# Rebuilding the set-up of a four-layer image kernel: core tables without a DRAM round trip, g on four row groups, small transfers first, aggregations per group of images

## The chip, the cores and the metric

The kernel runs on one core of a Trainium2 chip. Its time is the device time of one execution in microseconds (us), a median over runs. TensorE (PE) multiplies, VectorE (DVE), ScalarE (ACT) and GpSimd (POOL) work elementwise, and SyncE (SP) only issues transfers; ACT and POOL issue some as well. The order of the instructions on each engine is the one written in the kernel.

## The reference

The input `x` is 1024 images of 16 x 16 pixels and 16 channels, in float32. Four layers follow each other, each of the form `x = x + layer(group_norm(x))`, with 8 groups of two channels. Only the start of the first layer concerns this change:

```python
# _gn: mean and variance of an image's group (16 x 16 x 2 values)
x = x + _L0_conv_ref(_gn(x), core0, core1, core2)
# for each core r,o,i,k: einsum('roik,brix->bkox'); ranks 1,16,16,1; all dims 16
```

Layer 0 is thus one 4096 x 4096 matrix applied to every image, and that matrix is given by three small tensors: `core0` (16 x 16 x 16 values: o, i, k), `core1` (16 x 16 x 16 x 16) and `core2` (16 x 16 x 16). Layers 1 and 3 are a perception step with two dense layers, layer 2 is a 3 x 3 convolution.

## The kernel before, in words

The images are worked on in two sets of 512 (n = 0 and 1). Layer 0 runs on TensorE as 128 x 128 float32 matrices times 512 images. The matrix is cut into 2 x 2 blocks, which take seven products instead of eight (`PRODUCTS`), and the work is five phases of 16 units; phase 0 makes two products per unit of the first quarter with the first 512 images alone, and the second 512 images are read, turned and normalised beside it.

For a unit u the matrix `w` is built like this. `g` is the contraction of `core1` with `core2`; it is computed once, stored in DRAM (`g_dram`), and `gload(u)` reads 4 x 32 KB of it into `gq` (two buffers). `build(u)` multiplies `gq` with `R`, a table that spreads `core0` over partitions, on four groups of 32 rows (the `pw` matmuls), and ACT copies the four results into `w`. `mix(u, i)` adds parts of `w` on DVE for the products of phase 0 only the first of these. `pieces(u, k)` are the large matmuls `po`; between them it issues `build(u + 1)`, `gload(u + 2)` and the store of unit u - 1 (`m_dram`), so the order on all engines follows PE's.

The set-up ahead of phase 0 has two strands.

The input strand: SP loads x as eight 1 MB pieces (two halves of the rows, four groups of 128 images each; line 822). DVE takes `bn_stats` of each piece (line 834, eight instructions for a piece) and, in `small` (line 865), 32 `bn_aggr`. Then follow a square root on ACT, five small instructions (`newton`), two sets of four copies (`widen`, line 881), PE transposes of both (`spread`, `ptmr`, line 889), and ACT copies into `mr`. `normed` (line 911) subtracts the mean and multiplies by the reciprocal deviation, eight DVE instructions of 128 x 1024 for the first part. `turn` (line 840, `ptin`) transposes the images themselves, four transposes a row, and POOL stores the rows in DRAM as `xr` (lines 845 and 853).

The table strand (`train_setup`): ACT issues sixteen transfers of 16 KB for `core1` and one each for `core2` and `core0`. `cores` transposes `core1` in 32 transposes of 16 columns (line 522) into 16 partitions and `core0` in two. `sums` writes `core0` in masked form to DRAM (`c_dram`) and reads it back four times as `R`. `gs` multiplies 16 partitions of `core1` with `core2` (line 561, 32 matmuls for the first half of g), ACT copies (line 565), SP stores (line 570).

A transfer on SP's or ACT's path takes one of eight completion semaphores in turn, and waits at its issue until the former user of that semaphore has landed. So an issue on SP can wait for a transfer that ACT issued.

The order around the start is written out by hand:

```python
now(setup[:1])
now(stat[0] + stat[1] + lines[0][:4] + setup[1:] + tail[:1]
    + lines[1][:4] + tail[1:] + lines[0][4:10])
start, phases = layer_train()
start()          # gload(0), gload(1), build(0), mix(0, i), fetch(0)
now(normed(0, 0, 1) + combined(0, True))
```

Of the kernel before, what the change touches and what calls it, by code (L numbers as in the profile page):

```python
# [9 lines left out]
F32 = mybir.dt.float32  # L10
# [9 lines left out]
P = 128  # L20
# [83 lines left out]
def conv_preact_kernel(ctx: ExitStack, tc: tile.TileContext, a: dict, out: bass.AP):  # L104
# [31 lines left out]
    def work(shape, tag, name, dt=F32):  # L136
        p, sizes = pool["sb"]
        return p.tile(shape, dt, tag=tag, name=name, bufs=sizes[tag])
# [330 lines left out]
    c_dram = dram.tile([2, 16, 512], F32, tag="c_dram", name="c_dram")  # L469
# [27 lines left out]
    def train_setup(room):  # L497

        c1t = room[0:16, 0:4096].rearrange("p (h i w a k) -> p h i w a k", h=2, i=S, w=4, a=2)
        ra = [room[0:16, 4096 + 512 * a2 : 4608 + 512 * a2].rearrange("p (s m b f) -> p s m b f", s=2, m=2, b=2) for a2 in range(2)]  # L500
        c0 = room[0:16, 5888:6144].rearrange("p (i o) -> p i o", o=S)
        c1n = work([P, 2, NB], "t4", "core1")[:, 0].rearrange("p (t f) -> p t f", t=2)
        r = work([P, NB], "n", "cores")
        c2 = r[0:16, 0:256]
        c0n = r[:, 256:288].rearrange("p (t k) -> p t k", t=2)

        core1 = a["L0_conv_core1"].rearrange("k o i q -> o k (i q)")
        for h in range(2):
            for wv in range(4):
                for a2 in range(2):  # L510
                    A.dma_start(c1n[32 * wv + 16 * a2 : 32 * wv + 16 * a2 + 16, h], core1[8 * a2 + 4 * h + wv])
        A.dma_start(c2, a["L0_conv_core2"].rearrange("r o i k -> r (o i k)"))
        A.dma_start(
            c0n, a["L0_conv_core0"].rearrange("r o i k -> (r o i) k").rearrange("(t p) k -> p t k", p=P)
        )

        def cores():
            for h in range(2):
                for i2 in range(0, S, 4):
                    pt = bank([16, 4, P], "w", "pc1")  # L520
                    for j in range(4):
                        T.transpose(pt[:, j], c1n[:, h, 16 * (i2 + j) : 16 * (i2 + j) + 16], ident)
                    A.copy(c1t[:, h, i2 : i2 + 4].rearrange("p i w a k -> p i (w a k)"), pt)
            pt = bank([16, 2, P], "w", "pc0")
            for t in range(2):
                T.transpose(pt[:, t], c0n[:, t], ident)
            for t in range(2):
                A.copy(
                    c0[:, :, 8 * t : 8 * t + 8].rearrange("p i o -> p o i"),
                    pt[:, t].rearrange("p (o i) -> p o i", i=S),  # L530
                )

        def sums():
            c = c0.rearrange("p (b s t) o -> p s b (t o)", b=2, s=2)
            for a2 in range(2):
                G.memset(ra[a2], 0.0)
                G.tensor_copy(ra[a2][:, :, a2], c)
                G.dma_start(c_dram[a2], ra[a2].rearrange("p s m b f -> p (s m b f)"))

            st0["R"] = work([P, 2, 256], "R", "R")  # L540
            for g in range(4):
                G.dma_start(
                    st0["R"][32 * g : 32 * g + 32].rearrange("p s f -> p (s f)"),
                    c_dram.rearrange("a k f -> (a k) f"),
                )

        def gs(h, ih, o, ni, tag):


            if (h, ih, o) not in st0:  # L550
                if ih:
                    g = work([P, 2, NB], "t4", "g")
                else:
                    if o == 0:
                        st0["gw"] = work([P, 28, P], "w", "g")
                    g = st0["gw"][:, 8 * o : 8 * o + 8]
                st0[h, ih, o] = [g.rearrange("p m f -> p (m f)").rearrange("p (o f) -> p o f", o=8), 0]
            g, i2 = st0[h, ih, o]
            pg = bank([P, ni, 8, S], tag, "pg")
            for j in range(ni):  # L560
                T.matmul(
                    pg[:, j], c1t[:, h, 8 * ih + i2 + j].rearrange("p w a k -> p (w a k)"),
                    c2[:, P * o : P * o + P], start=True, stop=True,
                )
            A.copy(
                g[:, :, 16 * i2 : 16 * (i2 + ni)].rearrange("p o (j i) -> p j o i", j=ni), pg
            )
            st0[h, ih, o][1] += ni
            if i2 + ni == 8:
                nc.sync.dma_start(  # L570
                    g_dram[ih, 2 * h : 2 * h + 2, :, :, 8 * o : 8 * o + 8].rearrange(
                        "w v k o f -> (w v k) o f"
                    ),
                    g,
                )

        def all_gs(ih, tag):
            return [
                (1, lambda h=h, o=o: gs(h, ih, o, 4, tag)) for h in range(2) for o in range(2) for _ in range(2)
            ]  # L580

        return [cores, sums] + all_gs(0, "w"), all_gs(1, "mw")


# [227 lines left out]
    def input_steps(n, tag, lag, queue):  # L812
# [23 lines left out]
        def turn(h, wh):  # L836
            pt = bank([P, 4, P], tag[0], "ptin")
            for bg in range(4):
                x = slots[:, 4 * (h // 8) + bg].rearrange("p (h w f) -> p h w f", h=8, w=2)
                T.transpose(pt[:, bg], x[:, h % 8, wh], ident)  # L840
            pt = pt.rearrange("p g b -> p (g b)")
            if wh == 0 and h % 8 < 4:
                A.copy(X[:, h // 8, h % 4, 1], pt)
                if h % 4 == 3:
                    G.dma_start(
                        xr[n][0, h - 3 : h + 1].rearrange("h p b -> p h b"), X[:, h // 8, :, 1]
                    )
                return
            if h % 2 == 0:
                st["l"] = work([P, 2, NB], "t4", "lines")  # L850
            A.copy(st["l"][:, h % 2], pt)
            if h % 2 == 1:
                G.dma_start(
                    xr[n][wh, h - 1 : h + 1].rearrange("h p b -> p h b"), st["l"]
                )

        def small():
            t = work([P, NB], "n", "small")
            st["mv"] = t[:, 0:64].rearrange("p (g k e) -> p g k e", g=4, k=8)
            st["ve"], st["t"], st["r"] = (  # L860
                t[:, 64 + 32 * j : 96 + 32 * j].rearrange("p (g k) -> p g k", g=4) for j in range(3)
            )
            for bg in range(4):
                for g in range(8):
                    V.bn_aggr(st["mv"][:, bg, g], st["b"][:, bg, g])
            V.tensor_scalar(st["ve"], st["mv"][:, :, :, 1], GN_EPS, None, ALU.add)
            A.activation(st["t"], st["ve"], AF.Sqrt)
# [23 lines left out]

        loads = [lambda half=half, bg=bg: load(half, bg) for half in range(2) for bg in range(4)]
# [6 lines left out]
        tail = [(3, small), 2, (1, newton), (1, lambda: widen(0)), (1, lambda: widen(1)), 1]  # L899
        tail += [(0, lambda: spread(0)), lag, (0, lambda: spread(1)), 2]  # L900
        return loads, stat, lines, tail

    def normed(p, n, src=None):

        X, E = part_tile(p)

        def op(b, t, k):
            x = X[:, b, t : t + 2, n]
            y = x if k or src is None else X[:, b, t : t + 2, src]
            m = mr[:, k, n].unsqueeze(1).broadcast_to([P, 2, NB])  # L910
            V.tensor_tensor(x, y, m, ALU.mult if k else ALU.subtract)  # L911

        return [(1.2, lambda b=b, t=t, k=k: op(b, t, k)) for b in range(2) for t in (0, 2) for k in range(2)]
# [76 lines left out]
    def layer_train():  # L990
# [147 lines left out]
        def start():  # L1138
            gload(0)
            gload(1)  # L1140
            build(0)
            for i in range(5):
                mix(0, i)
            fetch(0)
# [5 lines left out]
        return start, steps  # L1150
# [381 lines left out]
    with ExitStack() as es:  # L1532
        stage(es, dict(gn, w=2, r=2, gq=2, R=1), dict(o=3, w=4, m=1))
        setup, later = train_setup(XN[0].rearrange("p n b -> p (n b)")[:, 8192:14336])
        tag = ["w"]
        loads, stat, lines, tail = input_steps(0, tag, 0, nc.sync)
# [3 lines left out]
        now(setup[:1])  # L1540
        now(stat[0] + stat[1] + lines[0][:4] + setup[1:] + tail[:1] + lines[1][:4] + tail[1:] + lines[0][4:10])
        start, phases = layer_train()
        start()
        now(normed(0, 0, 1) + combined(0, True))
        tag[0] = "mw"
        late = lines[0][10:] + lines[1][4:]
        loads, stat, lines, tail = input_steps(1, tag, 2, G)
        woven_in = [x for j in range(2) for i in range(4) for x in stat[j][i : i + 1] + lines[j][4 * i : 4 * i + 4]]
# [88 lines left out]
```

## Time and profile before

| What | Value |
|---|---|
| median of 3 runs | 3057.21 us (3052.56 to 3057.89) |
| profiled execution | 3054.15 us |
| its span, first to last instruction | 3052.4 us |
| PE busy | 2982.6 us, 98% of the span |
| DVE, ACT, POOL busy | 58%, 36%, 22% |
| mean granted TensorE clock | 0.988 |
| first large matmul (line 1098) begins | 50.13 us into the span |

In the rows of the timeline the first number is the start in us from the span's start, the second the time that the piece took; then come engine, line, operation, output and inputs, shapes, and in brackets how long the engine had idled before it and what ended that. A float32 matmul leaves two records, a transpose one. "issue" means that the profile shows nothing that the engine waited for. In rows by stretch each engine has its busy time, PEclk is the clock that TensorE was granted as a share of full speed, and the DMA share is the mean busy share of the 16 DMA engines.

### The profile page before, as it was taken

What the parts mean: (1) busy time and instruction counts of PE and PEld (TensorE: products, weight loads), DVE (VectorE), ACT (ScalarE), POOL (GpSimd) and SP (SyncE); (2) the same over time, 40 slices, a digit from 0 to 9 for tenths busy, and PEclk for the clock granted to TensorE, in tenths of its full rate; (3) what the DMA queues carried; (4) which work ended last, traced back from release to release, by engine and by line L of the source; (5) the groups of instructions that cost most, each with busy time, mean ns of one, the idle gap of its engine ahead of it and who ended that gap; (6) DMA issues with size and microseconds to landing.
All of it is one profiled execution on the core that took longest, in us unless ns stands there. A gap on an engine that the chain in (4) does not pass through costs nothing.

```text
span 3052.4 us, 36639 instructions
## 1 busy us (share of the span) xinstructions
PE 2982.6 (98%) x13746; PEld 1252.2 (41%) x13746; DVE 1757.4 (58%) x2338; ACT 1100.0 (36%) x1798; POOL 674.8 (22%) x732
## 2 busy tenths in 40 slices
PE   7999999999999999999999999999999999999996
PEld 5544334444444444444444433333333333333332
DVE  5254336555554555544555768756977766856432
ACT  4431341100000000000111156666667656666563
POOL 1114671200000000000000015434542223442331
PEclk8999999999999999999999999999999999999998
DMA  7642664533333433332222235436337866343555
GB/s 260 257 146 88 137 140 156 179 107 116 109 110 126 151 109 109 109 102 88 88 88 94 71 123 172 132 123 202 123 125 177 193 101 204 123 129 112 149 163 197
DMA packets 251809, 418.67 MB, mean 137 GB/s; under 512 B 35044, under 2 KB 105320, under 8 KB 248560
## 3 DMA queue, kind: packets, MB, share of 16 engines
q1 hardware_dynamic: 225376, 362.45, 35.9%
q0 software_dynamic: 25440, 53.58, 8.5%
q8 instruction: 109, 1.79, 0.2%
q14 instruction: 68, 0.56, 0.1%
q10 hardware_dynamic: 816, 0.30, 0.0%
HBM read 238.79 MB, written 165.60 MB: 132 GB/s over the span
## 4 chain that ended last, share of the span: by engine, by line
issue 47%; PE 43%; POOL 5%; DMA 1%; DVE 1%; ACT 0%; SPq 0%; POOLq 0%; DVEq 0%
PE ph L1466 17%; PE po L1098 13%; PE po L1317 6%; PE po L1193 2%; POOL u L1368 2%; POOL res L1369 2%; PE pw L1021 1%; PE L_conv_pe L392 1%; PE ptin L840 1%; POOL xf L1242 1%; PE ptx L1378 1%; DMA gq<-g_dram 0%; PE pr L739 0%; PE pvar L727 0%; PE pmean L723 0%
## 5 line engine op out<-in xcount | busy, mean ns | idle before, releaser
L1098 PE MATMUL po<-xn,w 128*128 128x512 f32 x3584 | 1577.4, 597 | 4.6 <-DVE xn L911 4.6
L1098 PEld LDWEIGHTS po<-xn,w 128*128 128x128 f32 x3584 | 672.3, 191 | 841.5 <-issue 818.3
L1469 ACT ACTIVATE hid<-ph,pack 128x512 f32<-128x512 f32 x1024 | 652.5, 686 | 380.5 <-PE ph L1466 271.0
L1134 DVE TENSOR_TENSOR r<-r,po 128x512 f32<-128x512 f32 x576 | 378.1, 684 | 577.0 <-PE po L1098 525.9
L1368 POOL TENSOR_TENSOR u<-u,mask 128x512 f32<-128x512 f32 x124 | 195.8, 1579 | 1817.4 <-DMA nx<-xn 1239.7
L1026 ACT COPY w<-pw 128x512 f32<-128x512 f32 (+1 forms) x320 | 150.6, 557 | 1214.4 <-issue 1014.5
L1466 PE MATMUL ph<-xn,wq 32*128 32x512 f32 x3664 | 565.7, 610 | 0.0
L1466 PEld LDWEIGHTS ph<-xn,wq 32*128 32x128 f32 x3664 | 232.8, 184 | 270.2 <-issue 238.2
L1466 PE MATMUL ph<-xn,pack 32*128 32x512 f32 x1288 | 297.5, 623 | 1.2 <-DVE mask L1362 0.9
L1317 PE MATMUL po<-hid,pack 128*32 128x512 f32 x2048 | 282.5, 606 | 2.7 <-ACT hid L1469 2.7
L1039 DVE TENSOR_TENSOR w<-w 128x512 f32<-128x512 f32 x320 | 210.5, 685 | 99.8 <-ACT w L1026 99.8
L640 DVE TENSOR_TENSOR xn<-xn,m 128x1024 f32<-128x1024 f32 x160 | 225.5, 1458 | 47.1 <-ACT m L655 47.0
L1329 DVE SCALAR_TENSOR_TENSOR u<-po,pack,xn 128x512 f32<-128x512 f32 x128 | 95.9, 749 | 204.7 <-PE po L1317 200.3
L1369 POOL TENSOR_TENSOR res<-res,u 128x512 f32<-128x512 f32 x124 | 207.5, 1673 | 9.7
L1193 PE MATMUL po<-xn,convw 128*128 128x512 f32 x368 | 166.8, 606 | 5.1 <-ACT conv L1241 5.1
L1466 PEld LDWEIGHTS ph<-xn,pack 32*128 32x128 f32 x1288 | 115.8, 185 | 98.4 <-issue 62.7
L1134 DVE TENSOR_TENSOR xn<-xn,po 128x512 f32<-128x512 f32 x96 | 64.4, 685 | 125.9 <-PE po L1098 125.8
L1317 PEld LDWEIGHTS po<-hid,pack 128*32 128x32 f32 x2048 | 43.1, 109 | 197.4 <-issue 137.7
L607 DVE TENSOR_TENSOR sq<-sq 128x1024 f32<-128x1024 f32 x78 | 106.9, 1370 | 13.1 <-ACT sq L625 10.8
L1193 PEld LDWEIGHTS po<-xn,convw 128*128 128x128 f32 x368 | 69.2, 193 | 102.1 <-issue 92.0
L404 POOL DMA_DIRECT2D L_conv_wy<-xn x160 | 88.8, 563 | 28.5 <-ACT xn L398 17.6
L1021 PE MATMUL pw<-R,gq 32*128 32x256 f32 (+1 forms) x1280 | 88.9, 383 | 2.3 <-DMA gq<-g_dram 2.3
(165 smaller groups left out, 1775.2 us busy)
## 6 DMA issues: line engine op xcount, KB each, us to landing
xf<-r SPq DMA_DIRECT2D x112, 512.0 KB, 3.9
xn<-xf SPq DMA_DIRECT2D x96, 512.0 KB, 5.0
r<-xf SPq DMA_DIRECT2D x80, 512.0 KB, 4.4
wq<-L_conv_wy SPq DMA_DIRECT2D x192, 192.0 KB, 2.7
res<-xf SPq DMA_DIRECT2D x128, 256.0 KB, 3.0
xf<-res SPq DMA_DIRECT2D x96, 256.0 KB, 2.0
res<-xr SPq DMA_DIRECT2D x256, 64.0 KB, 2.8
xf<-conv POOLq DMA_DIRECT2D x64, 256.0 KB, 6.0
```

Of the source, the lines that this page charges most:

```text
L640: V.tensor_tensor(part, part, m().unsqueeze(1).broadcast_to([P, 2, NB]), op)
L1021: T.matmul(pw[r][:, v], st["g", u][rows, v], st["R"][rows, p % 2, 64 * k0 : 256], start=True, stop=True,)
L1026: A.copy(w[:, k0:4, :, 32 * r : 32 * r + 32].rearrange("p k t (v o) -> p v (k t) o", v=2), pw[r],)
L1039: V.tensor_tensor(w[:, k], w[:, x], w[:, y], ALU.add if sign > 0 else ALU.subtract)
L1098: T.matmul(po, st["w", u][:, matrix, t], x, start=t == 0, stop=t == 3)
L1134: V.tensor_tensor(r[at], r[at], po, ALU.add if sign > 0 else ALU.subtract)
L1193: T.matmul(st["po", h][wh], conv["fw"][:, y], X[:, 16 * wh + h + y - 1], start=y == max(0, 1 - h), stop=y == min(2, S - h),)
L1317: T.matmul(po[32 * j : 32 * j + 32], nca["w1"][:, v], hid[j], start=v == 0, stop=v == 1)
L1368: by.tensor_tensor(u, u, st["m"][:, w2], ALU.mult)
L1369: by.tensor_tensor(r, r, u, ALU.add)
L1466: T.matmul(ph, w, x, start=k == 0, stop=k == len(tiles) - 1)
L1469: A.activation(h, ph, AF.Relu, bias=nca["bt"][:, r : r + 1])
```

## The change

- `core0` no longer goes through DRAM: DVE repeats it eight times along the free dimension, two transposes bring it to 128 partitions, and eight small ACT activations with a mask as scale write `R`.
- `core1` comes in eight transfers of 32 KB (four issued by ACT, four by POOL) in place of sixteen of 16 KB; POOL clears a tile and copies `core1` into it with gaps, and eight full transposes put it on four groups of 32 partitions (16 used in each). `core2` is loaded four times, once per group. The first half of g is then 16 matmuls of 256 columns on four row groups in place of 32 of 128 columns on one; the copies stay eight. The second half, woven into phase 0, has its matmuls on two row groups at a time and 16 smaller copies in place of eight.
- `core0` and the four `core2` transfers stand ahead of the eight loads of x on SP.
- `bn_aggr` is issued eight at a time behind the last four pieces' `bn_stats`; `widen(0)` and `spread(0)` come ahead of `newton`; in `normed` of the first part two subtractions come first, then `mix`, then the rest.
- Each store of g is followed by the reads that need it (`send`, `gload`); the two 1 MB stores of `xr` (`kept`) are issued later; sixteen image transposes (rows 4 to 7) move ahead of the statistics' end, and `build(0)` stands between the two `spread`.

```diff
-        return [cores, sums] + all_gs(0, "w"), all_gs(1, "mw")
+        nc.sync.dma_start(c0n, ...core0...)
+        for g in range(4):
+            nc.sync.dma_start(c2[32 * g : 32 * g + 16], ...core2...)
+        for wv in range(4):
+            for a2 in range(2):
+                (A if wv < 2 else G).dma_start(c1n[...], core1[...])
+        G.memset(room[:, 0:1024], 0.0)
+        for t in range(2):
+            V.tensor_copy(c0r[:, t], c0n[:, t].unsqueeze(1).broadcast_to([P, 8, S]))
+        def sums():
...
+            for t in range(2):
+                T.transpose(pt[:, t], c0r[:, t].rearrange("p n k -> p (n k)"), ident)
...
+                        A.activation(R[:, s, m, e], pt[:, s, e], AF.Identity, scale=al_c[:, m : m + 1])
         def cores():
+            for h in range(2):
+                G.tensor_copy(c1s[:, h, :, :, 0:16], c1n[:, h]...)
+            for h in range(2):
+                pt = bank([P, 4, P], "o", "pc1")
+                for x in range(4):
+                    T.transpose(pt[:, x], c1s[:, h, x]..., ident)
+                A.copy(c1t[:, h], pt)
+        def gmul(pg, h, ih, r, cols):
+            rows = slice(32 * r, 32 * r + 16)
+            for x in range(2):
+                T.matmul(pg[:, x], c1t[rows, h, 2 * ih + x], c2[rows, cols], start=True, stop=True)
+        def early(h):
+            pg = [bank([P, 2, 256], "w", "pg") for _ in range(4)]
+            for r in range(4):
+                gmul(pg[r], h, 0, r, slice(0, 256))
+            for r in range(4):
+                gput(gw[h], r, pg[r])
...
-        now(stat[0] + stat[1] + lines[0][:4] + setup[1:] + tail[:1] + lines[1][:4] + tail[1:] + lines[0][4:10])
-        start()
-        now(normed(0, 0, 1) + combined(0, True))
+        now([sums, cores] + stat[0] + stat[1] + lines[0][:4])
+        early(0)
+        early(1)
+        send(0, 0)
+        gload(0)
+        send(1, 0)
+        gload(1)
+        now(lines[0][4:8] + lines[1][:4] + tail[:2] + [spread0])
+        send(0, 1)
+        send(1, 1)
+        build(0)
+        now(tail[2:] + [spread1, kept] + lines[0][8:10])
+        fetch(0)
+        now(normed(0, 0, 1, [(0, 0, 0), (0, 2, 0)]))
+        mixed(0)
+        now(normed(0, 0, 1, [(0, 0, 1), (0, 2, 1), (1, 0, 0), (1, 2, 0), (1, 0, 1), (1, 2, 1)]))
+        now(combined(0, True))
```

## Prediction, made before the changed kernel ran

> **What bounds the kernel now.** I read the page first, then the stretches of the first 130 us, their timeline, the waits, and the chain. Of the page two lines matter:
>
> ```profile
> span 3052.4 us, 36639 instructions
> PE 2982.6 (98%) x13746; PEld 1252.2 (41%) x13746; DVE 1757.4 (58%) x2338; ACT 1100.0 (36%) x1798; POOL 674.8 (22%) x732
> ```
>
> PE is busy for nearly the whole span. A comparison of the two programs' instruction orders shows the same sequence on every engine from the end of phase 0 on. The change can therefore only move the moment at which PE starts its unbroken run, and what disturbs the first units. By stretch (start:end, length, then busy us and count of each engine, PEclk, DMA share, GB/s):
>
> ```profile
> 16.00:26.00 10.00, 10.00 (x77) 8.87 (x75) 7.14 (x22) 8.16 (x17) 3.29 (x6) 0.97 1.03 428
> 26.00:34.00 8.00, 8.00 (x38) 7.39 (x36) 6.33 (x22) 1.87 (x4) 0.49 (x1) 0.50 0.99 369
> 34.00:42.00 8.00, 3.90 (x20) 3.71 (x19) 4.59 (x45) 3.92 (x8) 2.78 (x5) 0.50 0.71 253
> 42.00:46.00 4.00, 3.58 (x32) 2.91 (x30) 0.00 (x0) 2.88 (x6) 2.15 (x3) 0.94 0.69 261
> 46.00:50.00 4.00, 0.00 (x0) 0.00 (x0) 2.97 (x4) 0.96 (x4) 0.00 (x0) 0.92 0.77 270
> 50.00:60.00 10.00, 9.38 (x32) 5.03 (x33) 9.90 (x10) 2.37 (x6) 0.72 (x1) 0.52 0.04 13
> 60.00:76.00 16.00, 16.00 (x79) 9.14 (x78) 0.83 (x2) 7.98 (x17) 4.35 (x8) 1.00 0.76 275
> ```
>
> From 50 us on PE is busy, but at half clock until 60. Before 50 it has two holes, at 34 to 38 and at 46 to 50. The timeline tells who makes them:
>
> ```profile
> 33.79 2.42 DVE L865 BATCH_NORM_AGGREGATE small<-bn 128x2 f32<-128x12 f32 x32
> 40.05 3.99 PE L840 MATMUL ptin<-ident,xn 128*128 128x128 f32 x24
> 43.97 1.61 PE L1021 MATMUL pw<-R,gq 32*128 32x128 f32 x16
> 46.99 0.69 DVE L1039 TENSOR_TENSOR w<-w 128x512 f32<-128x512 f32 x1 [7.87 <-ACT w L1026]
> 47.60 9.66 DVE L911 TENSOR_TENSOR xn<-xn 128x1024 f32<-128x1024 f32 x8
> 50.13 3.78 PE L1098 MATMUL po<-xn,w 128*128 128x512 f32 x4 [4.55 <-DVE xn L911]
> ```
>
> This is one chain: statistics end at 36.2, PE transposes until 44, `pw`, ACT's copies, `mix`, two of `normed`, first `po`. The statistics themselves wait for x, and x waits for the small loads that ACT issues:
>
> ```profile
> SPq L822 <- DMA core<-in_L_conv_core_dram: 11.4, 3, 5.5
> DVE bn L834 <- DMA xn<-in_x_dram: 7.4, 6, 2.4
> ```
>
> The last piece of x lands at 31.1. A second wait lies at unit 3, where the burst of x for the second 512 images (4 MB, issued by POOL from 65.5) holds up 128 KB of `gq`. In the chain of the first 100 us:
>
> ```profile
> 68.02 12.42 DMA gq<-g_dram
> ```
>
> **The change part by part.** All times are from the span's start in the profiled execution, which took 3054.15 us; that is 3.06 below the median.
>
> *Front.* `core0` is issued at 0.8, and the four `core2` follow at about 0.4 each, so x cannot be issued before 2.8. Its first piece also waits until `core0` has landed; the nearest rows, the two `cores` loads, took 1.7 and 3.4 us, so 2.5 to 4.2; I take 3.3. The first piece takes 5.5 as before (0.82 to 6.36): 8.8, a loss of 2.4. After that the lanes are free of `core1`, and a 1 MB piece takes 2.4 us at the 437 GB/s reached around 20 us. DVE needs 2.71 for a piece and 2.42/4 = 0.6 for a group's aggregation, so x keeps ahead and DVE becomes the bound: 8.8 + 8 x 2.71 + 2.42 = 32.9 in place of 36.2. Gain 3.3. If x flowed no better than before (31.1), it would be 31.1 + 2.7 + 0.6 = 34.4, gain 1.8; at the early end of `core0`, gain 4.1. DVE's two copies of `core0` run while it waits for x and cost nothing.
>
> *From the statistics to the first `po`.* Before: 50.13 - 36.2 = 13.9. Now 0.2 (epsilon) and 0.6 (`widen(0)`) lead to `ptmr` at 33.7; four transposes at half clock 1.0, ACT's copy 0.6, giving 35.3; two subtractions 2.4, 37.7. Beside them PE does `pw` (1.6 at half clock, to 36.3) and ACT four copies of 0.3 (37.5). `mix` 0.7 gives 38.4, one multiplication 1.2 gives 39.6. On PE the second `ptmr` and eight `ptin` take 1.0 + 2.0 behind `pw` and end at 39.3, under DVE's. So `po` begins at 39.6: 6.7 for 13.9, a gain of 7.2. Of it 4.0 are the 24 `ptin`, of which 16 moved ahead, and 2.4 the subtractions taken out from behind `mix`. Front and this together: 10.5.
>
> *Whether PE has room for what moved ahead.* Piece 4 of x lands near 16. From there PE has 16 `ptin`, the 16 g matmuls, and 32 `ptin`. A block of 16 takes 1.9 at full clock (18.93 row) and 3.9 at half. The g matmuls on four row groups are not in the trace: as well interleaved as `pw` of 256 columns (16 records 1.15) their 32 records would take 2.3; in their written order each group's four records come in a row, so only the last overlaps the next group, 32 x 0.213 x 3/4 = 5.1 at full clock, 10.2 at half. The sum is 8 to 11 or, at half clock throughout, 21.9, ending at 38, 4 us after `ptmr` could start. ACT's eight copies (0.59 each, 4.7) hide under PE. I charge 1.0, since the clock was 0.97 in 16 to 26 and I expect part of the stretch at full speed; bounds 0 and 4.
>
> The 26:34 row shows PE busy all the time and yet the clock at 0.50: 16-row weights (line 561) filled the 10 us before. The 42:46 row shows it back at 0.94 after 5.6 us in which PE ran nothing but transposes. The Trainium skill, "TensorE: Matmul & The Clock Gate", Part 4, says that transposes do not count as busy for the clock; here they did. By the page everything until `po` would be at half clock, the charge 4 rather than 1, and the gain 3 us smaller.
>
> *g's way to `pw`.* The first store now waits for ACT's fourth copy (22 to 27), stands behind x on SP's queue, and the reads of `gq` wait for it. Stores took 6.4 to 10.4 before, with two to three pieces of x ahead of the first; now one or two are. Landing at 29 to 37, four issues at 0.4, landing of the read 2.5 to 3.9: 33 to 42.6, where `pw` is wanted at 34.7. I take 35.7, near the short end because less of x lies ahead: cost 1.0, bounds 0 and 8. Behind a late `pw` stand the second `ptmr`, all `ptin` and `po` on PE, so a late read is paid in full. `R` no longer passes through POOL's queue, where it landed at 39.6; it needs two transposes and eight ACT instructions near 9 us, in time nobody waits for.
>
> *Clock after `po`.* From 50 to 59.7 PE ran at half clock, which cost 4.8. PE had stood still for 4.5 us ahead of it. Now it is busy with `pw`, `ptmr`, `ptin` in the 5 us before. Full clock at once gives 4.8 less DVE's limit (the last `normed` ends at 45.6, so about 4); the same pattern as before gives 0. I take 2.
>
> *Second half of g.* 64 records of 128 columns in phase 0 took 0.128 each, 8.2; two row groups in turn overlap one in eight: gain 0 to 1, and 16 smaller copies on an ACT that is under half busy. I take 0. The aggregations of the second images cost nothing, since DVE has 0.83 of 16 us of work in the 60:76 row. The two `kept` stores, issued at 22 and 39 before, now follow POOL's first two line stores, from about 27; nobody reads them soon, and the DMA share of 0.04 at 50 to 60 shows that the engines have time. If they meet g's store and reads, 2 MB at 420 GB/s are 5 us, within the bound above.
>
> *The burst.* It is tied to the sixth line store, and so to PE's own progress. It moves with `po`, and unit 3 waits as before: 0, bounds minus 6 and plus 6.
>
> Sum: 10.5 - 1 - 1 + 2 = 10.5. The profiled execution and the three runs average 3055.4; 3055.4 - 10.5 = 3045 us.
>
> **The rivals.**
>
> *A larger gain.* Clock full from the first `po`, no charge for room and g, and unit 3's `gq` served between the bursts (2.3 us of idle PE in 76 to 82, and 6.8 us at half clock after it, 3.4): 10.5 + 2 + 2 + 5.7 = 20.2, 3035. For it speaks that nothing idles ahead of `po`; against it that the burst is tied to PE's progress.
>
> *g read at the head of PE's queue (the other side).* The first store leaves at 27, takes 10.4 like the longest one, the reads take 10.9 like those of unit 3: 27 + 10.4 + 1.7 + 10.9 = 50; `pw`, `ptmr`, copy and `normed` 4.4 more: first `po` at 54.4, and `gq` of unit 1, queued behind, 2 late: 3055.4 + 6.3 = 3062. It decides once the last read of unit 0 lands after 45.7. Against it: the 10.9 was under a 4 MB burst, which does not exist then. A milder form (read at 42) leaves 4 of gain, 3051.
>
> *The set-up is shorter but the gain does not arrive.* If phase 0's pace came from the second images' loads and normalising, the end would not move: 3055. The 60:76 row, PE 16.00 of 16.00 with DVE at 0.83, speaks against it.
>
> **How the numbers follow.** Forecast 0.60; larger gain 0.15; late g read 0.17, of which 0.07 reaches beyond before; gain lost 0.08. About 0.2%, 6 us, is what a measurement of this kernel tells from no change. Faster, below 3051, are the forecast, the larger gain and part of the late read: 0.78. The same: 0.15. Slower: 0.07. The range takes the larger gain at its lower end, 3035, and at its upper the mild late read and half the runs' spread of 5.3, 3051 + 2.7, rounded up with the case of the gain lost to 3055.
>
> **What would show it.** Last `bn_stats` beginning near 29.6 and ending with its aggregation at 32.9, DVE not waiting after the first piece; first `po` at 39 to 43 instead of 50; `pw` of unit 0 waiting less than 2 us on `gq`; the granted clock in the 10 us after the first `po` above 0.52; unit 3 still waiting 3 to 5 us for `gq`. I would be wrong if DVE's `bn` waits for x go on, if `gq` of unit 0 lands after 42, or if the end of phase 0 does not move with `po`.

## The result, and the profile after

The changed kernel took 3048.3 us, the median of 12 runs (3043.75 to 3050.82), beside 3057.78 us (3052.52 to 3061.36, 12 runs) for the kernel before: a ratio of 0.997, with a 95% interval of 0.9963 to 0.9978. That is 9.5 us less, where 10.5 were forecast. The profiled execution took 3044.7 us.

From the page of the changed kernel, the span and the busy times:

```profile
span 3043.0 us, 36508 instructions
PE 2971.3 (98%) x13690; PEld 1238.6 (41%) x13690; DVE 1760.2 (58%) x2340; ACT 1099.7 (36%) x1806; POOL 675.3 (22%) x729
```

PE is as full as before and is busy for 11.3 us less. By stretch, with the columns of the rows shown before (start:end, length, busy us and count of PE, PEld, DVE, ACT and POOL, PEclk, DMA share, GB/s):

```profile
16.00:26.00 10.00, 9.81 (x48) 7.88 (x49) 9.85 (x44) 6.39 (x12) 0.00 (x0) 1.00 1.00 416
26.00:34.00 8.00, 5.66 (x41) 5.31 (x39) 7.86 (x42) 5.02 (x11) 3.01 (x4) 1.00 0.60 226
34.00:42.00 8.00, 6.25 (x39) 4.09 (x40) 7.86 (x13) 3.13 (x8) 0.71 (x1) 0.79 1.03 397
42.00:46.00 4.00, 3.73 (x28) 2.53 (x28) 4.00 (x5) 2.61 (x7) 0.73 (x1) 1.00 0.59 218
```

DVE is now busy almost without a break from 16 to 46 (9.85 of 10, 7.86 of 8 twice, 4.00 of 4): it has become the bound of the set-up, as the front's step had it. PE has gaps in the 26:34 row, so it does have room for what moved ahead of the statistics' end. The clock column needs care here: this profile has no record of the clock before 28.43, and where there is none the rows read 1.00. The image transposes tell more: they follow each other every 213 ns until 28.4 and every 109 ns after that, so PE worked at half clock until then, through the first of these rows and into the second. The hole of 46 to 50 is gone. The timeline names the links of the chain:

```profile
31.71 0.70 DVE L882 BATCH_NORM_AGGREGATE small<-bn 128x2 f32<-128x12 f32 x8
32.90 0.64 PE L908 MATMUL ptmr<-ident,wide 128*128 128x128 f32 x4 [2.34 <-DVE wide L900]
33.48 1.45 PE L1046 MATMUL pw<-R,gq 32*128 32x128 f32 x16
34.97 2.35 DVE L935 TENSOR_TENSOR xn<-xn 128x1024 f32<-128x1024 f32 x2
37.24 0.68 DVE L1064 TENSOR_TENSOR w<-w 128x512 f32<-128x512 f32 x1
37.84 6.90 DVE L935 TENSOR_TENSOR xn<-xn 128x1024 f32<-128x1024 f32 x6
39.12 1.98 PE L1123 MATMUL po<-xn,w 128*128 128x512 f32 x4 [1.14 <-DVE xn L935]
```

The statistics end at 32.41 (36.21 before), `ptmr` follows 0.5 later, `pw` directly behind it without a wait for `gq`, and the first `po` starts at 39.12 instead of 50.13. In the chain of the first 100 us, unit 3 still waits for its g under the burst:

```profile
53.31 13.21 DMA gq<-g_dram
```

The times below are us from each span's start; a unit's end is the start of ACT's copy of its second result, and the last station is the start of ACT's last instruction on `hid`, in layer 3. The last column is a second profile of the same changed kernel (`after_again` below).

| Station | before | after | gain | after, again |
|---|---|---|---|---|
| last aggregation ends | 36.21 | 32.41 | 3.8 | 32.38 |
| first `po` | 50.13 | 39.12 | 11.0 | 39.08 |
| unit 0 ends | 65.56 | 50.82 | 14.7 | 52.50 |
| unit 1 ends | 74.59 | 59.85 | 14.7 | 61.54 |
| unit 3, first result | 97.00 | 83.00 | 14.0 | 85.14 |
| unit 15 ends (end of phase 0) | 218.74 | 206.56 | 12.2 | 208.70 |
| last `hid` on ACT | 3024.14 | 3014.23 | 9.9 | 3016.6 |

So the set-up gave 11.0, the first unit another 3.7, and 4.8 went again on the way to the end. The experiments were to say what of the 11.0 belongs to which part, and where the 4.8 went. Since the total of one execution varies by 7 to 9 us for the same kernel, the parts are read at these stations, of which those of the set-up repeat far better: the first `po` to 0.04 us in the two profiles of the changed kernel. The later ones differ by 1.7 to 2.4 there, with the clock.

### The profile page after: what moved, and what is told of

Read it like the earlier page. It is cut to its first block, busy times and chain, and to the rows that moved or that the text cites. A ratio compares the mean times of both kernels' runs of the same rounds, so it can differ in the third digit from the quotient of the medians.

```text
span 3043.0 us, 36508 instructions
## 1 busy us (share of the span) xinstructions
PE 2971.3 (98%) x13690; PEld 1238.6 (41%) x13690; DVE 1760.2 (58%) x2340; ACT 1099.7 (36%) x1806; POOL 675.3 (22%) x729
## 4 chain that ended last, share of the span: by engine, by line
PE 80%; issue 10%; POOL 6%; DMA 2%; DVE 1%; ACT 1%; SPq 0%; POOLq 0%; DVEq 0%; ACTq 0%
PE po L1123 51%; PE ph L1488 16%; PE po L1339 6%; PE pw L1046 3%; POOL res L1391 2%; POOL u L1390 2%; POOL xf L1264 2%; PE ptin L855 1%; PE L_conv_pe L392 1%; DMA gq<-g_dram 1%; PE ptx L1400 1%; PE pvar L742 0%; PE pmean L738 0%; PE pg L554 0%; DMA xn<-in_x_dram 0%
```

## Experiments on the set-up

All edits are on the changed kernel, each profiled once. Their single times (agg_end 3050.11, mix_first 3047.34, split_undone 3054.92, c1_act16 3053.56, c2_on_act 3047.56, r_dram 3045.89, interleaved 3049.30, and those named below) decide little beside a spread of 7 to 9 us, and the stations are read instead.

**The image transposes stay behind the statistics** (only rows 0 to 3 of either half ahead of them, as before; `newton` and the second `spread` come ahead of `build(0)` again as well):

```diff
-        now(lines[0][4:8] + lines[1][:4] + tail[:2] + [spread0])
+        now(lines[1][:4] + tail[:2] + [spread0])
...
+        now(tail[2:] + [spread1] + lines[0][4:10])
         build(0)
-        now(tail[2:] + [spread1, kept] + lines[0][8:10])
+        now([kept])
```

> The changed kernel with the sixteen image transposes of rows 4 to 7 back behind both spread, and so ahead of pw and build(0), 24 transposes in a row as before. Theory (what stands between the statistics and pw is paid in full on PE): 24 transposes in place of none ahead of pw, 2.9 us at full clock and 5.8 at half, so pw from 38 to 41 and the first po at 42.5 to 45.5. Rival (DVE's chain and the read of g hide them): first po at 39 to 40.

Timeline of this kernel:

```profile
35.40 4.60 PE L855 MATMUL ptin<-ident,xn 128*128 128x128 f32 x24
39.93 1.55 PE L1046 MATMUL pw<-R,gq 32*128 32x128 f32 x16
44.42 2.93 PE L1123 MATMUL po<-xn,w 128*128 128x512 f32 x3 [2.95 <-DVE xn L935]
```

The 24 `ptin` stand between the second `ptmr` and `pw` again, and PE then idles 2.95 for DVE, whose `mix` waits for the `pw` behind them. First `po` at 44.42, 5.3 later, and phase 0 ends at 213.72, 7.2 later (5.0 against the second profile). This is the largest single part. Some of it is the clock of this execution, at half from 32.28 to 39.10: at the 1.91 us that 16 `ptin` took at full clock in the kernel before, 24 would take some 2.9 in place of 4.60 (an estimate), so about 1.7 of the 5.3. Time 3054.11, one run.

**`mix` ahead of all of `normed`** (no subtraction in front of it):

```diff
-        now(normed(0, 0, 1, [(0, 0, 0), (0, 2, 0)]))
         mixed(0)
-        now(normed(0, 0, 1, [(0, 0, 1), (0, 2, 1), (1, 0, 0), ...]))
+        now(normed(0, 0, 1))
```

> The changed kernel with one thing undone: mix stands ahead of the eight normed instructions again, in their old order. Theory of the prediction (the two subtractions were taken out of the path, worth 2.4): the first po starts 2.4 later, at 41.5. Rival (from the timeline after: ACT's copies of w end at 35.96, so mix would end at 36.7, and one subtraction and one multiplication at 39.1): the first po starts at 39.1 as now, its second half needs 41.4 instead of 40.2, and PE reaches the end of unit 0 (second r copy, now 50.8) within 0.5 us of that.

Timeline:

```profile
36.14 0.69 DVE L1064 TENSOR_TENSOR w<-w 128x512 f32<-128x512 f32 x1 [0.94 <-ACT w L1051]
39.36 1.98 PE L1123 MATMUL po<-xn,w 128*128 128x512 f32 x4 [2.49 <-DVE xn L935]
47.68 1.98 PE L1123 MATMUL po<-xn,w 128*128 128x512 f32 x4 [1.55 <-DVE xn L956]
```

DVE idles 0.94 for ACT's copies and then has `mix`, one subtraction and one multiplication ahead of `po`, in place of two subtractions, `mix` and one multiplication: `po` at 39.36, 0.24 later, in which the statistics' own end (32.56 for 32.41) accounts for 0.15. So for the first `po` the order of `mix` and the subtractions is worth about 0.1, not 2.4. But the idle time comes back behind it: DVE ends `normed` at 46.48 instead of 44.74, PE then waits 1.55 for DVE (the last row), and unit 0 ends at 52.29 instead of 50.82, although the clock was full from 31.43 to 68.97. So neither side of the expectation held there: the order is worth some 1.5 at the end of unit 0. At the end of phase 0 it no longer shows (206.72 for 206.56); the stretch at half clock near unit 3 was 3.4 us shorter in this execution.

**The two halves of the mean and deviation together** (both `newton`, both `widen`, then both `spread` ahead of `build(0)`):

```diff
-        now(lines[0][4:8] + lines[1][:4] + tail[:2] + [spread0])
+        now(lines[0][4:8] + lines[1][:4] + [tail[0], tail[3], tail[1], tail[4], spread0, spread1])
...
-        now(tail[2:] + [spread1, kept] + lines[0][8:10])
+        now([kept] + lines[0][8:10])
```

> The changed kernel with the square root and newton ahead of both widen, and both spread ahead of build(0), as before. Theory (pw then stands behind the reciprocal deviation's chain): pw of unit 0 at 36 instead of 33.5, first po 1.2 to 2 later, at 40.4 to 41.2. Rival (DVE's normed set the start of po, pw has slack): first po at 39.1 +- 0.5.

Timeline:

```profile
34.55 1.94 PE L908 MATMUL ptmr<-ident,wide 128*128 128x128 f32 x8 [3.82 <-DVE wide L900]
41.12 2.93 PE L1123 MATMUL po<-xn,w 128*128 128x512 f32 x3 [0.72 <-DVE xn L935]
```

`ptmr` starts 1.65 later, because the square root and `newton` (33.01 to 34.2 on DVE) stand ahead of the first wide copies; `po` 2.0 later. DVE's first subtraction starts 1.3 later (36.29), and `mix` then waits 0.59 more for ACT's copies of `pw`, which PE ran at half clock (32.97 to 50.04 in this execution). So the early `spread(0)` is worth 2.0 here, of which 1.3 stand in DVE's own chain.

**The aggregations at the end again**, as 32 in one row:

```diff
-        now([sums, cores] + stat[0] + stat[1] + lines[0][:4])
+        now([sums, cores] + stat[0] + stat[1][0::2] + stat[1][1::2] + lines[0][:4])
```

> The changed kernel with one thing undone: the 32 bn_aggr of the first images stand together behind the last bn_stats, as before. Theory (DVE is the bound from the first piece of x on, since x lands faster than DVE can read it): the place of the aggregations does not matter, their work only moves; the last aggregation ends within 0.5 us of the 32.4 of the changed kernel, the first po starts at 39.1 +- 0.6. Rival (x is the bound, as it was before, and the aggregations filled DVE's waits): the statistics end 1.8 to 2.1 later, at 34.3, and the first po starts at 41.

Timeline:

```profile
29.98 2.42 DVE L882 BATCH_NORM_AGGREGATE small<-bn 128x2 f32<-128x12 f32 x32
39.18 1.22 PE L1123 MATMUL po<-xn,w 128*128 128x512 f32 x1 [0.80 <-DVE xn L935]
```

They end at 32.40 either way, and `po` starts at 39.18. DVE works without a break here, so where its 2.42 us of aggregations stand makes no difference. They would help only where DVE waits for the last piece of x.

**`core1` in sixteen transfers, all issued by ACT:**

```diff
-                (A if wv < 2 else G).dma_start(c1n[...], core1[8 * a2 + wv : 8 * a2 + wv + 5 : 4]...)
+                for h in range(2):
+                    A.dma_start(c1n[..., h], core1[8 * a2 + 4 * h + wv])
```

> The changed kernel with core1 in sixteen transfers of 16 KB, all issued by ACT, as before; core0 and core2 stay ahead of x on SP. Theory (SP's loads of x wait at their issue for ACT's core1 loads that hold the same completion semaphores): SP stands 5 to 11 us in those waits again, DVE waits for x again, the last aggregation ends at 34 to 35 and the first po starts 1.5 to 2.5 later than 39.1. Rival (only the order on SP counts, and x keeps ahead of DVE anyway): the last aggregation ends at 32.4 and the first po starts at 39.1 +- 0.6.

Its waits from 0 to 62 us (what waited, for what, us in all, times, longest):

```profile
SPq L837 <- DMA core<-in_L_conv_core_dram: 5.6, 2, 3.8
DVE bn L849 <- DMA xn<-in_x_dram: 5.8, 3, 3.4
```

SP's queue is held up by `core1` again (11.4 before), and DVE waits 5.8 for x, where the changed kernel waited once, for 2.2. The statistics end at 34.85 and `po` starts at 41.55, 2.4 later. That is the larger part of the front's 3.8.

**`core2` on ACT's queue** in place of SP's (`nc.sync.dma_start` becomes `A.dma_start` for the four loads):

> The changed kernel with the four core2 loads issued by ACT instead of SP, so that only core0 stands ahead of x on SP. Theory (DVE is the bound from the first piece on, so what brings the first piece brings everything): first bn_stats at 7 to 7.9 instead of 8.8, last aggregation and first po earlier by the same 0.9 to 1.8. Rival (x then waits at its issue for ACT's loads that hold the completion semaphores): first bn_stats not earlier, or later pieces late, first po at 39 or after.

The first `bn_stats` starts at 7.61, 1.2 earlier, but SP then waits 3.4 for tables (2.4 for `core1`, 1.0 for `core0` and `core2`) and 4.5 for a piece of x, and the statistics end at 32.60, `po` starts at 39.48:

```profile
SPq L837 <- DMA xn<-in_x_dram: 4.5, 1, 4.5
```

The early start of x is lost at later pieces.

**`R` through DRAM** (computed as in the changed kernel, stored, and read back; `cores` ahead of `sums`):

```diff
-            R = st0["R"] = work([P, 2, 256], "R", "R")
+            Rt = work([P, 2, 256], "s", "Rt")
...
+            G.dma_start(r_dram, Rt...)
+            G.dma_start(st0["R"]..., r_dram)
```

> The changed kernel with R once more through DRAM: the eight activations write a work tile, POOL stores it and reads it back as R (256 KB each way, in one piece). Theory (R is needed at 33.5 only and is ready near 9, so its way costs nothing unless it takes over 24 us): pw of unit 0 at 33.5 +- 0.5, first po at 39.1 +- 0.7. Rival (POOL's queue and the loads of x make it late, as it was before at 39.6): pw after 35, the first po later by as much.

Store and read took 7.1 and 6.4 us, and still `pw` started at 33.30, not later than the changed kernel's 33.48; `po` at 39.54, 0.4 later, with half clock from 33.3 to 40.1 in this execution. A single round trip of `R`, early, cost at most that here. What delayed `pw` in the kernel before was PE's order, not the table: `R` landed at 39.6 and `pw` began at 43.97, straight behind `ptin`. By these times, with the new order alone the 39.6 would have been the next bound.

**g's first half in interleaved order** (row groups 0, 1, 2, 3, then again, in place of 0, 0, 1, 1, ...):

```diff
-            for r in range(4):
-                gmul(pg[r], h, 0, r, slice(0, 256))
+            for x in range(2):
+                for r in range(4):
+                    T.matmul(pg[r][:, x], c1t[rows, h, x], c2[rows, 0:256], start=True, stop=True)
```

> The changed kernel with the sixteen g matmuls of the set-up in the order group 0, 1, 2, 3, 0, 1, 2, 3 in place of 0, 0, 1, 1, 2, 2, 3, 3. Theory (two matmuls of one row group behind each other overlap only at their ends): PE's g matmuls take 2.5 to 4 in all in place of the 6.3 between 19.16 and 25.44, unless ACT's copies hold them; the first po does not move (39.1 +- 0.6), since PE waits 2.3 for DVE ahead of ptmr anyway. Rival (the order does not matter): 6.3 as now.

Timeline of this kernel:

```profile
19.40 1.87 PE L576 MATMUL pg<-cores,xn 16*128 16x256 f32 x16
21.53 3.42 PE L576 MATMUL pg<-cores,xn 16*128 16x256 f32 x16 [0.26 <-ACT xn L557]
```

The first eight matmuls took 1.87, in the profile of the changed kernel 2.81. But that is the clock and not the order: the 2.81 fell in the stretch at half clock before 28.4, and with the order unaltered the same eight take 1.87 where the clock is up, as in burst_spread (an edit that comes in far later, described below):

```profile
19.63 1.87 PE L554 MATMUL pg<-cores,xn 16*128 16x256 f32 x16
```

They take 1.87 in flip, r_dram and split_undone too, and 1.96 in the second profile of the changed kernel. The second eight took 3.42 here, with half clock from 23.15, and 3.25 in burst_spread, with half clock from 23.38. Both together took 5.5 in place of the 2.5 to 4 expected. So the rival held: no effect of the order shows. `po` did not move either (39.22): PE has room here.

Undone one by one, the parts make `po` later by 5.3 (transposes), 2.4 (`core1`), 2.0 (early `spread`), 0.1 (`mix`) and 0 (aggregations). That these come to 9.8 of the 11.0 is no account of it: the first and the third both put `newton` and the second `spread` ahead of `pw` again and so overlap, and both hold some half clock. Which part the rest belongs to was not isolated.

## Experiments on what was given back

**The banks turned by one.** In phase 0 `pw` takes PSUM banks of the kind "w", and `ptin` and g's second half take one of the kind "m" and one of the kind "w" alternately (`bank` flips a bit, `either`, each time). Where a `ptin` directly behind `pw` falls on "w", it waits until ACT has copied that bank out. How the alternation falls depends on all that was taken before, and the change altered it. PE's waits from unit 1 to the end of phase 0, in the kernel before (62 to 210 us):

```profile
PE ptin L840 <- ACT w L1026: 1.3, 3, 0.4
```

and in the changed kernel (62 to 200):

```profile
PE ptin L855 <- ACT w L1051: 3.1, 7, 0.4
PE pg L554 <- ACT g L557: 2.2, 3, 0.8
```

The edit flips the bit once before phase 0, and nothing else:

```diff
         tag[0] = "mw"
+        either[0] ^= 1
```

> The changed kernel with one more turn of the switch that gives woven matmuls the PSUM bank of its own or one of the four shared with pw, ahead of phase 0; nothing else moves. Theory (the 2 us lost between unit 4 and unit 12 are transposes that stand directly behind pw and fall on a shared bank, so that PE waits 0.44 for ACT's first copy of w: 9 of 10 such places in the changed kernel, 2 of 10 here): PE's waits of ptin for ACT's w fall from 3.1 to under 1 us, and from the end of unit 3's pw to the second r copy of unit 15 takes 136.3 to 137.2 instead of 138.7. Rival (the loss comes from the woven order itself or from g's second half): it stays at 138.2 to 139.

PE's waits of that kernel, 62 to 206 us:

```profile
PE ptin L855 <- ACT w L1051: 0.4, 1, 0.4
```

From unit 3's first result to the end of unit 15 the kernel before took 121.74, the changed kernel 123.56 in both its profiles (and 123.56 to 123.58 in agg_end, mix_first, turns_first, c1_act16, c2_on_act, r_dram, split_undone and interleaved), and flip 120.63. The `ptin` waits that went (2.7) are nearly as much as the 2.93; `pg`'s waits for ACT fell as well, from 2.6 to 1.4, and 0.5 came at `ptmr`. The station of the expectation took 134.79 for 138.71, even less than the 136.3 to 137.2 expected, but it holds a stretch at half clock that was 3.4 us shorter in flip; from unit 3's first result on both are at full clock. So the change gave back about 1.8 by an alternation of banks that no line of the diff shows, and one line wins it back with 1.1 more. Time 3038.18, one run.

**The burst spread out:** the first three of the eight loads of x for the second images are issued four entries of the woven list apart in place of four at once, the other five together later.

```diff
-            (late[:6] + loads[0:4] + late[6:] + loads[4:] + ...
+            (late[:6] + [loads[0]] + late[6:10] + [loads[1]] + late[10:14] + [loads[2]] + late[14:] + loads[3:] + ...
```

> The changed kernel with the first four 1 MB loads of the second images spread over twelve woven steps instead of standing together. Theory (unit 3's gq is late because it shares the DMA engines with that burst): PE waits for gq under 1 us, unit 3's pw ends at 62 to 64 instead of 67.85, no half clock around 66, the second r copy of unit 3 comes 5 to 6.5 earlier relative to the first po. Rival (gq is late behind the m_dram store on SP's queue and the line stores): pw ends at 66 to 68 as now.

Timeline of this kernel:

```profile
63.18 1.88 PE L1123 MATMUL po<-xn,w 128*128 128x512 f32 x4
64.99 0.73 PE L1046 MATMUL pw<-R,gq 32*128 32x128 f32 x16
```

Unit 3's sixteen `pw` records take 0.73 and follow `po` at once, where in the changed kernel they came in four portions as `gq` landed. PE waits for nothing from 55 to 80, and no half clock follows. From the end of unit 0 to unit 3's first result it took 24.97 in place of 32.18: 7.2. (Unit 3's `pw` ended at 65.72, past the 62 to 64 expected, because unit 0 had ended 1.75 later in this execution.) Phase 0 ended at 201.22, against 208.70 in the profile of the changed kernel with the same end of unit 0 (52.5). The kernel before took 31.44 there, so the burst's price was some 7 us in the changed kernel and, if it can be spread as well there, some 6.5 in the kernel before; that was not run. Time 3041.92, one run.

**Both, and g's second half on the "w" banks alone** (in `gs`, `"mw"` becomes `"w"`), and beside it the changed kernel again, without an edit:

> Three edits on the changed kernel: the bank switch turned once more (flip), the burst of loads spread (burst_spread), and g's second half on the four shared banks alone, so that its third product need not wait for the single bank. Theory (the three losses found are independent): no wait for gq at unit 3, ptin waits under 1 us, pg waits for ACT under 0.5 us instead of 2.2; second r copy of unit 15 at 194 to 198 against 206.6, and a median 8 to 12 us below the changed kernel run beside it. Rival (PE then waits elsewhere, or the clock takes it back): less than 5.

> The changed kernel itself, unaltered. Theory (the half-clock stretches lie on a grid of 3.41 us that runs freely against the program, and decide what is left of the gain): from the second r copy of unit 15 on, where the two programs are the same, the time to the end differs from the first profile by 0.5 to 4 us, by about half of the difference in half-clock time; up to unit 15 it is within 2.5 us of 206.6. Rival (what is lost after phase 0 belongs to the change): the rest of the span repeats within 0.3 us. Timed: 8 to 11 us below the kernel before.

The combined kernel took 3042.67 (3034.59 to 3046.27, 5 runs), a ratio to before of 0.9949 (0.9935 to 0.9962); the changed kernel again 3048.98 (3043.95 to 3051.52, 9 runs), 0.9972 (0.9962 to 0.9982); before 3057.52 (13 runs). So it beats both, by 6.3 and 14.9, but not by the sum of its parts: the expectation of 8 to 12 below the changed kernel failed, and so did the rival's less than 5. The waits of `ptin` (0.9) and of `pg` (0.4) are as small as expected, but its phase 0 ended at 200.74 in place of 194 to 198, hardly earlier than with the spread burst alone (201.22). Its chain and its timeline show what took the gain:

```profile
89.91 7.93 DMA gq<-g_dram
```
```profile
97.98 1.75 PE L1046 MATMUL pw<-R,gq 32*128 32x128 f32 x16 [2.95 <-DMA gq<-g_dram]
```

The last five loads now start at 74.67 to 77.33, a later unit's g reads land behind them, PE waits 2.95 and half clock follows for 6.8 from 97.1. From unit 3 to unit 15 it took 123.44 in place of flip's 120.63. In burst_spread the same five loads start at 74.91 to 77.57 and the same reads land no earlier (98.87 for 97.84), but PE gets to that `pw` later, at 99.23, and does not wait. The wait was moved two or three units on, not removed; whether the loads or g's 512 KB stores on SP's queue hold the reads up there was not separated.

**The last piece: the clock after phase 0.** From unit 15 on the instructions stand in the same order in all these kernels, yet this rest (unit 15's end to the last `hid` on ACT) took 2805.4 in the profile of before, 2807.7 in that of after, and up to 2813.4. With it goes the time at half clock inside the rest:

| kernel | half clock, us | rest, us |
|---|---|---|
| before | 17.1 | 2805.4 |
| flip | 17.1 | 2805.8 |
| after | 20.5 | 2807.7 |
| after_again | 20.5 | 2807.9 |
| r_dram | 23.9 | 2810.2 |
| agg_end | 27.3 | 2811.0 |
| best2 | 27.3 | 2813.0 |
| c1_act16 | 30.7 | 2813.4 |

Over all 14 profiles a straight line gives 0.59 us for each us at half clock (correlation 0.95); half speed alone would give 0.5. All half-clock stretches in the rest are multiples of 3.41 us, and in each run they start on one grid of 3.41 us, whose phase differs from run to run. The Trainium skill, "TensorE: Matmul & The Clock Gate", Part 1, "What's actually happening", describes this: a free-running window of 3413 ns that does not start with the kernel. For modeling it puts the ramp's penalty below 1% of a typical kernel's span and advises against fitting a count of cold matmuls; here 8 us of 2808 are 0.3%, and nearly as large as the effect that was measured. That the phase decides how many windows of the rest fall to half clock fits all profiles, but no run set the phase, so it is argued, not shown. The second profile of the changed kernel could not decide it: its rest took 2807.9 for 2807.7, with the same time at half clock, so the expected difference of 0.5 to 4 us did not come, and the rival's 0.3 did. The kernel before has one profile; whether the change itself has a part in the 2.3 us lost between these two stays open.

## Why the prediction was right, step by step

*Front.* Predicted 3.3, measured 3.8. First `bn_stats` at 8.83 (8.8 predicted), last aggregation's end at 32.41 (32.9). DVE became the bound. The wait of the first piece for `core0` is not seen: SP issued it at 3.20, straight behind the five small ones, so the 3.3 came out right for another reason. The gain came for the most part from the transfers (c1_act16: 2.4), not from moving the aggregations (agg_end: 0); the other 1.4 were not isolated.

*From the statistics to the first `po`.* 39.6 predicted without the charges, 39.12 measured: right in sum, wrong in its attribution. Of the 7.2, 4.0 were given to the 24 `ptin`; undone, they cost 5.3, with the clock and the second `spread` in it. The sentence that 2.4 came from "the subtractions taken out from behind `mix`" failed. Before, only one subtraction of 1.2 lay between `mix` and the first `po` (two of the eight `normed`, 47.60 to 50.13); now two stand ahead of `mix`, in DVE's own chain, and mix_first shows 0.1 at the first `po`. In its place stands the early `spread(0)`, 2.0 (split_undone), which the step followed in time but did not price.

*Whether PE has room.* 1.0 charged, 0 measured, and not because the clock was up: PE was at half clock until 28.4 and still idled 2.34 ahead of `ptmr`. What the step had wrong is the price of g's matmuls, 10.2 at half clock because only the last record of a group would overlap the next one; they took 6.28 at half clock, waits for ACT included. On transposes and the clock, turns_first bears the row of before out. Two of its stretches:

```profile
38.00:39.00 1.00, 1.00 (x6) 1.00 (x5) 0.00 (x0) 0.59 (x1) 0.75 (x1) 0.50 0.00 0
39.00:41.00 2.00, 2.00 (x22) 1.59 (x22) 0.00 (x0) 1.66 (x3) 0.73 (x1) 0.97 0.68 262
```

From 35.4 on PE ran only `ptin`, and the clock went from 0.50 to 0.97 in the midst of it. In the changed kernel's profile too it rose, at 28.43, after 3 us of `ptin` alone. The page's rule cited in the prediction would have held it at half.

*g's way to `pw`.* 1.0 charged, 0 measured: the first store left at 23.34, the reads were issued from 28.22 on, before the 29 to 37 given for the store's landing, and had landed by 32.4; `pw` started at 33.48 without a wait.

*Clock after `po`.* 2 predicted. From the first `po` to unit 0's end: 15.43 before, 11.70 after, 13.42 in the second profile, so 3.7 or 2.0, with the clock: in the first profile a stretch at half clock ended at 38.7, ahead of `po`, in the second one from 34.1 lasted to 44.3. The clock is not all of it: at full clock mix_first took 12.93, so the subtractions ahead of `mix`, which this step did not count, bring some 1.2 here. Two stretches of the second profile:

```profile
34.00:42.00 8.00, 6.96 (x26) 4.51 (x26) 7.86 (x13) 3.09 (x8) 0.71 (x1) 0.51 1.03 395
42.00:46.00 4.00, 3.56 (x28) 2.24 (x27) 4.00 (x5) 1.96 (x6) 0.00 (x0) 0.71 0.39 143
```

*Second half of g.* 0 predicted, about 0 found, by two effects that cancel: its 64 records kept PE busy for 5.76 in place of 8.19, and PE waited 2.2 for ACT's copies of them (the `pg` row above), which it had not done before. No run undid this part alone.

*The burst.* 0 predicted, a loss of 0.7 measured (the gain of 14.7 at unit 1's end is 14.0 at unit 3's first result); the wait of 13.21 in the chain moved along with `po`, as said. The prediction named it and priced the wait and the half clock behind it at 2.3 + 3.4; burst_spread shows 7.2.

*Not in the sum:* the bank alternation, 1.8 lost, and the clock in the rest, 2.3 lost between the two profiles that were compared.

So the account between the profiled executions is: 11.0 at `po`, 3.7 in unit 0, less 0.7 at the burst, less 1.8 from unit 3 to unit 15, less 2.3 in the rest and 0.5 behind it: 9.4, the difference of the two spans. Against the terms of the sum this is 0.5 more at `po`, 2 for the two charges that did not come and 1.7 more in unit 0, 4.2 in all, and 5.3 of losses that stood in the sum at 0 or not at all. That these nearly cancel is luck; that `po` moved by 11 where 10.5 were worked out for it is not. Of the 3.3 us between 3045 and the median, 2.4 come from the starting value, 3055.4, which is lower than the 3057.78 measured beside the changed kernel. The range held it.

*The rivals.* The larger gain had its conditions half met: no charges, and the clock up early in one profile; its burst part stayed away, and the banks and the rest's clock took what was left. The late read of g was far off: `pw` was there 12 us before the 45.7 from which it would have decided. That the gain does not arrive was wrong: the end of phase 0 moved by 12.2, or by 10.0 in the second profile.

## What to carry to other kernels

On a chain of several engines, find out by undoing one link what each is worth: here the transposes parked ahead of a critical matmul and one engine's transfers holding up another's queue made most of the gain, one reordering on an engine that was busy anyway gave nothing, and another nothing at the first `po` but 1.5 us at the end of the unit behind it, so look further down than the link. Parts undone one at a time overlap and need not add up. After a change in the set-up, look at which buffers the steady part now gets: a shift by one in an alternation of banks cost 1.8 us here. And where single executions of one kernel differ by some us, compare stations inside the trace, not totals, and profile the same kernel twice before a difference is explained. A duration on TensorE is compared only beside the clock it ran at: the order of g's matmuls seemed to be worth a third of their time until the same time was found without it.

## What the runs showed of the hardware

- The TensorE clock changed in steps of 3.41 us on a grid whose phase differed per run. The same instructions after phase 0 took 2805.4 to 2813.4 us, and the same first unit, from `po` on, 11.70 and 13.42.
- Eight float32 matmuls of 16 rows and 256 columns on four row groups took 2.81 us at half clock and 1.87 at full clock; with the groups alternating, 1.87 as well.
- Transposes alone brought the clock from half to full (`ptin` from 35.4 in turns_first, clock up at 39.1; from 25.4 in the changed kernel, up at 28.43). With 16-row matmuls alone it fell to half (kernel before: from 20.77 on, half from 25.45).
- 32 KB reads issued just behind a burst of 4 MB took 10.1 to 13.2 us to land; with the burst's pieces apart they took 7.4 to 7.7, and PE did not wait.
- A transposed group directly behind `pw` on a bank whose copy was still under way cost PE about 0.44 us each time (3.1 for seven).
